# Reciprocal standard deviations in a perceiver kernel: a power on GpSimd in place of ScalarE's root and VectorE's reciprocal

## The chip, the cores and the metric

The kernel runs on one core of a Trainium2 chip, as one program. The metric is the device time of one execution in microseconds (us); lower is better. Five engines work side by side, each with its own queue of instructions in a fixed order: TensorE (PE, with PEld for its weight loads), VectorE (DVE), ScalarE (ACT), GpSimd (POOL) and SyncE (SP, which issues most DMAs). An instruction that depends on another engine waits on a semaphore, and everything behind it in its queue waits too.

## The reference

The input x is 2 x 256 rows of 256 values; a context has 2 x 4096 rows. Twelve sublayers follow one another, each a residual step on the normalised x:

```python
def _layernorm(x, axis=-1, eps=1e-05):
    m = jnp.mean(x, axis=axis, keepdims=True)
    v = jnp.var(x, axis=axis, keepdims=True)
    return (x - m) / jnp.sqrt(v + eps)
...
    x = x + _L0_xattn_ref(_layernorm(x, axis=-1), ctx_1024, ...)
    x = x + _L0_attn_ref(_layernorm(x, axis=-1), ...)
    x = x + _L0_ffn_ref(_layernorm(x, axis=-1), ...)
...
    x = x + _L3_ffn_ref(_layernorm(x, axis=-1), ...)
```

The sublayers are cross attention over the context, self attention, gated and expert feed-forward layers, a state-space layer (l1_attn), an int8 linear layer and a long convolution by Fourier transforms (l2_xattn). Some have norms of their own: the convolution normalises its context projection (twice, once per batch), its query and its gated result (twice); l2_ffn has two RMS norms, `x * rsqrt(mean(x * x) + eps) * w`; l3_attn a layer norm. Each of them needs 1 / sqrt(v + eps) for every row.

## The kernel before

The 512 rows of x lie on the chip as four tiles of 128 rows (partitions) by 256 values. A norm works on a whole tile set: VectorE's `bn_stats` and `bn_aggr` give mean and variance of each row, so the variances of four tiles are a small array of 128 partitions by 4 columns. `rstd` turns it into reciprocal standard deviations `r`: VectorE adds epsilon (L367), ScalarE takes the root in place (L368), VectorE takes the reciprocal (L370). Then VectorE scales the rows with `r`, one column per tile (L384 in `layernorm`), and TensorE transposes the result (L435) for the matmuls. The convolution calls `rstd` on 8 columns (`normalise`) and on 2 columns (`gate`). `norm_of_norm` and `enter` call it twice in a row, because a layer norm is followed directly by another norm: the second variance is worked out from the first one.

That makes twenty calls. By the start of L367 in the profiled execution they stand at 6.6 us (l0_xattn), 140.0 (l0_attn), 229.7 (l0_ffn), 266.3 (l1_xattn), 1248.1 (l1_attn), 1428.0 (the int8 layer), 1455.6 (`normalise(0)`), 1474.7 and 1475.7 (`enter`), 1480.0 (`normalise(1)`), 1517.3 (`gate(0)`), 1535.7 (`gate(1)`), 1547.8 (l2_attn), 1618.0 and 1621.6 (first norm of l2_ffn, a norm of a norm), 1704.4 (its second, `rmsnorm`), 1839.5 (l3_xattn), 2274.5 and 2275.6 (l3_attn), and 2390.3 (l3_ffn).

ScalarE evaluates functions from tables. When the next function is of another set than the one loaded, the compiler puts an ACT_TABLE_LOAD ahead of it in ScalarE's queue. Exp, Silu and the root are each of a set of their own here; copies and Identity need no load.

The order of each engine's instructions is made by a planner when the kernel is built: it simulates the program and, where several instructions are ready on an engine, prefers the one that comes first in the program. Where the author wants another order, `with self.in_order(...)` chains the instructions of the named engines in the order in which they are written. The first cross attentions, the state-space layer and the int8-and-convolution stage name Pool (GpSimd) too; in the other stages GpSimd's order is the planner's.

Between the sublayers TensorE is given other work where there is some: keys and values that later layers need are computed early (`fill`, `early`, `ahead`). ScalarE or VectorE moves their results out of the accumulators (L931, L959, L963), and a DMA stores them (L932, L967).

Names that the prediction's steps touch:
- Convolution stage: L1688 (a maximum over the normalised x of the int8 layer), L1702 (GpSimd, x plus bias), L1776 (filter taps), L1808 (`less`, minus mean times `r`), L1824 (spectrum times filter), L1722 (gain and shift), L1729 (Silu of its feed-forward), L1872, L1884 and L1885 (GpSimd, residual sums).
- Exp and Silu elsewhere: L549 (Exp in l0_xattn), L770 (a dummy Exp that loads the table early, in three self attentions), L1546 (Exp in l1_attn), L1993 (Exp in the router of l2_ffn), L2632 (Exp in l3_attn).
- GpSimd: L457 (x plus a row), L1320 and L2479 (running sums of attention weights), L1455 (a polynomial's first step), L1596 (a product in the state-space layer, read by L1609 on VectorE), L2236 (a sum whose input is VectorE's L2235), L1981 (an iota for the router), L2160 (indirect DMA that sends rows to experts), L2397 (clears a padded tile in l3_xattn).
- L439: gain on a transposed norm.

## Time and profile before

| | |
|---|---|
| time, median of 3 runs (lowest to highest) | 2505.35 us (2504.6 to 2508.54) |
| profiled execution: time, span of its instructions | 2506.37 us, 2504.6 us |
| TensorE busy, granted clock over the span | 2408.0 us (96%), 0.983 |
| VectorE, ScalarE, GpSimd busy | 1691.9 us, 1347.6 us, 912.1 us |
| L367, median of one | 171 ns (16 of the 20) |
| L368, the root, median of one | 206 ns, 20 times |
| L368, table loads | 14 of 1283 ns |
| L370, the reciprocal, median of one | 178 ns, 20 times |
| table loads in all | 32 |

Busy shares are averages over stages with different limits; whether a norm costs time is seen only where it stands. The views used are the page (busy times, the chain of work that ended last, the costliest groups), the view of one source line (durations, what it waits for and who waits for it), the chain in order of time, and the timeline of an engine. In the chain, "issue" is time in which the engine waited for nothing that the profile shows. Times in these views are microseconds from the start of the span.

### The profile page before, as it was taken

The page shows a single profiled execution, that of the slowest core. Times are in us where ns is not written, and L with a number is a line of the kernel's source. Part 1 is how long each engine was busy: PE and PEld are TensorE (multiplying, and loading weights), DVE is VectorE, ACT ScalarE, POOL GpSimd, SP SyncE. Part 2 cuts the span into 40 slices and gives each one's busy share as a digit, 9 for nine tenths or more (in the row PEclk, how much of TensorE's full clock was granted, in tenths as well). Part 3 has the DMA queues.
Part 4 walks back from the last instruction along what each step waited for, and adds up shares of the span by engine and source line. Part 5 has one row for each costly group of instructions (what it writes and reads, how often), then busy time and mean ns, then how long its engine had stood idle before and what let it go on. Part 6 is the DMA issues. An engine that isn't in the chain of part 4 may idle for free.

```text
span 2504.6 us, 51328 instructions
## 1 busy us (share of the span) xinstructions
PE 2408.0 (96%) x20501; PEld 1609.6 (64%) x20501; DVE 1691.9 (68%) x3077; ACT 1347.6 (54%) x2556; POOL 912.1 (36%) x856
## 2 busy tenths in 40 slices
PE   8999999999999999999899998999979999999989
PEld 6865477777766666666633465556945666665678
DVE  5555588888877777777669755554268888854642
ACT  3334576666666666666467422432215777785612
POOL 0520066666666666665539512001011222210010
PEclk9999999999999999999999999999988999999989
DMA  7221433333342222222310102126830000003656
GB/s 301 97 98 67 140 100 96 98 98 94 100 130 69 70 70 71 70 69 69 126 60 1 68 17 97 60 77 216 312 128 1 2 2 2 2 2 136 220 237 218
DMA packets 92638, 243.60 MB, mean 97 GB/s; under 512 B 8072, under 2 KB 23248, under 8 KB 81904
## 3 DMA queue, kind: packets, MB, share of 16 engines
q1 hardware_dynamic: 81088, 219.08, 26.4%
q10 hardware_dynamic: 8784, 13.24, 1.4%
q0 software_dynamic: 2528, 8.00, 0.9%
q8 instruction: 162, 2.65, 0.5%
q14 instruction: 76, 0.62, 0.1%
HBM read 206.87 MB, written 33.42 MB: 96 GB/s over the span
## 4 chain that ended last, share of the span: by engine, by line
PE 89%; DVE 5%; ACT 2%; DMA 2%; issue 1%; POOL 0%; another core or an unknown queue 0%; ACTq 0%; SPq 0%; DVEq 0%; POOLq 0%
PE ps_tr L1238 15%; PE ps_mm L359 13%; PE ps_mm L1285 10%; PE acc L1332 9%; PE ps_tr L2470 5%; PE ps_mm L2430 5%; PE ps_tr L2454 5%; PE acc L359 4%; PE ps_tr L359 2%; PE acc L563 2%; PE acc L1618 2%; PE ps_mm L823 2%; PE ps_mm L1238 2%; DVE mx L2415 1%; PE ps_mm L1577 1%
## 5 line engine op out<-in xcount | busy, mean ns | idle before, releaser
L1320 POOL TENSOR_TENSOR total<-total,S 128x512 f32<-128x512 f32 x434 | 543.1, 1284 | 227.5 <-ACT S L1309 227.0
L1309 ACT ACTIVATE S<-S 128x512 f32<-128x512 f32 x512 | 304.1, 626 | 209.2 <-DVE S L1306 209.0
L1295 DVE TENSOR_TENSOR most<-ps_mm,most 128x512 f32<-128x512 f32 x448 | 278.1, 683 | 101.1 <-ACT S L1292 101.1
L1306 DVE TENSOR_TENSOR S<-S,ps_dec 128x512 f32<-128x512 f32 x512 | 317.3, 678 | 1.7 <-PE ps_dec L1367 1.7
L2434 DVE TENSOR_REDUCE mx<-ps_mm 128x1 f32<-128x512 f32 x448 | 278.1, 683 | 52.1 <-PE ps_tr L2454 48.2
L1292 ACT COPY S<-ps_mm 128x512 f32<-128x512 f32 x512 | 262.4, 598 | 73.2 <-PE ps_mm L1285 73.1
L2458 ACT ACTIVATE PT<-ps_tr 128x512 f32<-128x512 f32 x476 | 246.9, 601 | 82.1 <-PE ps_tr L2454 78.9
L1238 PEld LDWEIGHTS ps_tr<-w_l1x_wv,ctxT 128*64 128x64 f32 x4096 | 236.9, 138 | 46.3 <-issue 41.6
L1285 PE MATMUL ps_mm<-qT,kT 64*128 64x256 f32 x2048 | 256.6, 389 | 0.8 <-DVE qT L1244 0.8
L1332 PE MATMUL acc<-S,v 128*64 128x256 f32 x2048 | 252.2, 385 | 1.7 <-ACT S L1309 1.0
L1238 PE MATMUL ps_tr<-w_l1x_wv,ctxT 128*64 128x128 f32 x4096 | 249.6, 273 | 0.0
L2454 PE MATMUL ps_tr<-qm,kT 32*128 32x256 f32 x1904 | 240.2, 391 | 0.0
L2430 PE MATMUL ps_mm<-kT,qT 32*128 32x512 f32 x896 | 228.9, 627 | 2.9 <-DVE mx L2415 2.7
L1285 PEld LDWEIGHTS ps_mm<-qT,kT 64*128 64x128 f32 x2048 | 188.5, 186 | 44.6 <-issue 12.2
L1332 PEld LDWEIGHTS acc<-S,v 128*64 128x64 f32 x2048 | 139.5, 136 | 96.3 <-ACT S L1292 33.8
L1238 PE MATMUL ps_tr<-ctxT,w_l1x_wk 128*64 128x512 f32 x800 | 189.6, 593 | 0.0
L2454 PEld LDWEIGHTS ps_tr<-qm,kT 32*128 32x128 f32 x1904 | 172.7, 185 | 16.4 <-issue 6.2
L2479 POOL TENSOR_TENSOR sums<-sums,part 128x256 f32<-128x256 f32 x102 | 73.9, 724 | 250.5 <-ACT part L2478 250.5
L2470 PE MATMUL ps_tr<-PT,v 128*32 128x256 f32 x2048 | 139.4, 385 | 0.0
L336 DVE COPY v<-ps_tr 128x512 f32<-128x512 f32 x120 | 82.4, 687 | 44.1 <-PE ps_tr L1238 44.1
L2430 PEld LDWEIGHTS ps_mm<-kT,qT 32*128 32x128 f32 x896 | 80.6, 187 | 48.0 <-issue 41.1
L1238 PEld LDWEIGHTS ps_tr<-ctxT,w_l1x_wk 128*64 128x64 f32 x800 | 59.7, 137 | 70.5 <-issue 58.9
(578 smaller groups left out, 3832.8 us busy)
## 6 DMA issues: line engine op xcount, KB each, us to landing
ctxT<-in_ctxT SPq DMA_DIRECT2D x144, 512.0 KB, 3.6
w_l2f_gu<-in_l2f_gu SPq DMA_DIRECT2D x16, 1024.0 KB, 7.1
bd_dram<-bd SPq DMA_DIRECT2D x8, 1536.0 KB, 6.0
w_l3f_w<-in_l3f_w SPq DMA_DIRECT2D x11, 1028.0 KB, 10.6
w_l3f_w<-in_l3f_w SPq DMA_DIRECT2D x11, 1024.0 KB, 6.8
ctxT<-in_ctxT SPq DMA_DIRECT2D x8, 1024.0 KB, 6.2
ctx<-in_ctx SPq DMA_DIRECT2D x8, 1024.0 KB, 4.8
ahead_ctx<-in_ctxT SPq DMA_DIRECT2D x8, 1024.0 KB, 5.7
```

Source lines behind the costliest of these rows:

```text
L359: self.nc.tensor.matmul(out, lhsT, rhs, start=i == 0, stop=i == len(pairs) - 1)
L1238: nc.tensor.matmul(ps[part], a[:, part], b, start=k == 0, stop=k == len(pairs) - 1)
L1285: nc.tensor.matmul(banks[hh, i][:, j, :], k[part, ts(2 * i + j, P)], q[u][part, :], start=True, stop=True)
L1295: nc.vector.tensor_tensor(m, ps, m, ALU.max)
L1306: nc.vector.tensor_tensor(t, t, spread[u][:, hh, :].unsqueeze(1).to_broadcast([P, 2, L]), ALU.add)
L1309: nc.scalar.activation(t, t, AF.Exp)
L1320: nc.gpsimd.tensor_add(tot, tot, t)
L1332: nc.tensor.matmul(av[u][part], vs[:, 2 * i + j, part], got[hh, i][:, j, :], start=g % 8 == 0 and i + j == 0, stop=g % 8 == 7 and i + j == 2,)
L2430: nc.tensor.matmul(ps, qT[rows, 2 * half + c, ts(t, P)], kT[rows, ts(j, 512)], start=True, stop=True,)
L2434: nc.vector.tensor_reduce(mx[:, c, r, j : j + 1], ps, AX.X, ALU.max)
L2454: nc.tensor.matmul(ps[:, i, :], kT[rows, ts(2 * u + i, P)], q[rows], start=True, stop=True)
L2470: nc.tensor.matmul(ps[ts(r, 32), :], v[:, 2 * u + i, :], pt[:, i, :], start=i == 0, stop=i == 1)
```

## The change

A constant tile of minus one half is written once by VectorE at the start. In `rstd` the sum of variance and epsilon is still made on VectorE, and then GpSimd raises it to the power minus one half in one two-input instruction. ScalarE's root and VectorE's reciprocal are gone, and with them the root's table set. All twenty calls change.

```diff
@@ in Perceiver.__init__
         nc.vector.memset(self.ones, 1.0)
+        self.minus_half = self.const.tile([P, 8], F32, name="minus_half")
+        nc.vector.memset(self.minus_half, -0.5)
         self.ternary = {}
@@ rstd
         nc, n = self.nc, var.shape[1]
-        s = self.sm.tile([P, n], F32, name="std", tag=f"std{n}")
-        nc.vector.tensor_scalar_add(s, var, eps)
-        nc.scalar.sqrt(s, s)
         r = self.sm.tile([P, n], F32, name="rstd", tag=f"rstd{n}")
-        nc.vector.reciprocal(r, s)
+        v = self.sm.tile([P, n], F32, name="std", tag=f"std{n}")
+        nc.vector.tensor_scalar_add(v, var, eps)
+        nc.gpsimd.tensor_tensor(r, v, self.minus_half[:, 0:n], ALU.pow)
         return r
```

## The prediction

> **What bounds the kernel now.** I read the page first: the busy times and the chain that ended last.

> ```profile
> PE 2408.0 (96%) x20501; PEld 1609.6 (64%) x20501; DVE 1691.9 (68%) x3077; ACT 1347.6 (54%) x2556; POOL 912.1 (36%) x856
> ...
> PE 89%; DVE 5%; ACT 2%; DMA 2%; issue 1%; POOL 0%; another core or an unknown queue 0%; ACTq 0%; SPq 0%; DVEq 0%; POOLq 0%
> ```

> TensorE carries 89% of the chain. The change touches no matmul, so it can act only in the few places where TensorE stands still for a norm. ScalarE is no bound (54% busy), so time taken off it is not time gained. Next, the root's own line, L368:

> ```profile
> L368 ACT ACTIVATE std<-std x20: 203/206/208, 6.8 to 2390.5; 128x4 f32<-128x4 f32 x16, 128x8 f32<-128x8 f32 x2, 128x2 f32<-128x2 f32 x2
> L368 ACT ACT_TABLE_LOAD  x14: 1283/1283/1283, 3.4 to 2385.3; - x14
> ```

> Twenty norms on 2, 4 or 8 columns, and 14 table loads. Then the chain in order of time, around each of the twenty. Columns are start, length, who:

> ```profile
> 1474.70 0.18 DVE std L367
> 1474.88 0.02 issue
> 1474.90 0.21 ACT std L368
> 1475.12 0.02 issue
> 1475.14 0.19 DVE rstd L370
> 1475.33 0.02 issue
> 1475.35 0.17 DVE both L1865
> ```

> This is the common form: from the end of the addition of epsilon (L367) to the end of the reciprocal (L370) 0.45 us, with no table load, because the load was already done while ScalarE idled. Only in a few places is the load itself in the chain, as here before l1_attn:

> ```profile
> 1247.64 1.28 ACT L368
> 1248.92 0.01 issue
> 1248.93 0.21 ACT std L368
> 1249.15 0.02 issue
> 1249.17 0.19 DVE rstd L370
> ```

> Here L367 had ended at 1248.22, and the reciprocal ends at 1249.35, 1.13 us later. Last, GpSimd: its rows by form, and its timeline at 1480 us.

> ```profile
> L1320 POOL TENSOR_TENSOR total<-total,S 128x512 f32<-128x512 f32 x434 | 543.1, 1284 | 227.5 <-ACT S L1309 227.0
> L2479 POOL TENSOR_TENSOR sums<-sums,part 128x256 f32<-128x256 f32 x102 | 73.9, 724 | 250.5 <-ACT part L2478 250.5
> L2160 POOL DMA_INDIRECT xs<-xn,slot x12 | 12.1, 1005 | 32.7 <-DVE own L2193 16.1 <-DVE near L2253 13.5 <-issue 3.0
> L1455 POOL TENSOR_SCALAR delta<-low 128x512 f32<-128x512 f32 x2 | 3.0, 1510 | 0.0
> ```

> ```profile
> 1478.43 2.92 POOL L1872 TENSOR_TENSOR add<-add,row_l2x 128x256 f32<-128x256 f32 x4 [18.00 <-issue]
> ```

> **The price of one power.** No row of before shows a power. From below: two-input GpSimd instructions take 724 ns for 256 columns and 1284 ns for 512, so 2.19 ns a column and 0.16 us fixed; four columns of the cheapest operation would be 0.17 us. From above I take the longest GpSimd instruction of the page, 1.51 us. [...] I take 1.0 us for four columns. Scaling what lies over the fixed part, that is 0.6 us for two columns and 1.85 us for eight.

> Handing over: L2236 on GpSimd starts 0.08 us after its VectorE input L2235 ends; L1609 on VectorE starts 0.03 us after L1596 on GpSimd ends. So L367's end to r ready costs 0.11 us plus the power: 1.11 us where 0.45 us was.

> **Removed: table loads.** The 14 loads of the root go. So do 9 more, because without the root the function before was already of the wanted set: L549 (1), L770 (2 of 3), L1546 (1), L1729 (3), L1993 (1), L2632 (1). That leaves 9 of 32. 23 x 1.283 = 29.5 us of ScalarE time, which would be the gain if each were waited for. [...] The trace shows why that is not the gain: most loads begin as soon as ScalarE is idle and end before their input comes. Of the 9 others only one is in the chain, L1729 at 1540.46, and TensorE, still working until 1542.11, resumes at 1542.28: worth 0.17 us.

> **Place by place**, at 1.0 us a power. r means the norm's result.
> - Seven four-column norms on the chain in the common form (6.6, 140.0, 1428.0, 1474.7, 1475.7, 1547.8, 2390.3 us): each 1.11 - 0.45 = +0.66, sum +4.6. The one at 1428 isn't named in the chain, but VectorE goes straight on from it through L1688 to L1776, which the chain has.
> - Two of two columns (1517.3, 1535.7): 0.71 - 0.44 = +0.27 each, +0.5.
> - Eight columns at 1455.6: 1.96 - 0.48, +1.5.
> - Eight columns at 1480.0: in this stage GpSimd's order is written by hand, and the power stands behind the four L1872, which end at 1478.43 + 2.92 = 1481.35, while L367 ended at 1480.70. So r at 1481.35 + 1.85 + 0.03 = 1483.23 instead of 1481.18: +2.05. Queued behind it on VectorE are L1808, L1824 and L1722, for which TensorE waits.
> - 1248.1: 1248.22 + 1.11 = 1249.33 against 1249.35, 0. 1839.5, the same picture: 1839.63 + 1.11 = 1840.74 against 1840.70, 0. The load saved pays for the power.
> - 1704.4 (RMS norm): ScalarE's copy L963, which releases TensorE, no longer stands behind load and root. It can start with its input at 1704.92 instead of 1705.50: -0.6.
> - 1618.0 and 1621.6 (norm of a norm): the first root waits for load and copies, 2.70 us instead of 0.45. But GpSimd clears tiles from 1617.51 to 1620.46. If the first power starts midway at 1619.5, r is there at 1620.5; then 0.60 us as before to the second L367's end and 1.11: 1622.2, as before: 0. Ends -1.6 (no wait, cheap power; TensorE is busy until 1621.4) and +1.0.
> - Off the chain at no cost: 229.7 and 266.3 (TensorE computes early keys; r has about 0.7 and 3.6 us of room), 2274.5 and 2275.6 (TensorE projects positions until 2280.9, about 2.3 us of room). If a power took over 2 us, that cover is gone and they count too.
> - GpSimd already busy with clearing or counting when the power comes, at 140, 1547 and 2390: up to 0.5 us each for the instruction in flight; half of that, +0.75 in all.
> - The constant's memset, 0.1 us at the start on an idle VectorE: 0. L1702, L1884 and L1885, which the power now precedes on GpSimd, have many microseconds before their readers: 0.

> Sum: 4.6 + 0.5 + 1.5 + 2.05 + 0 - 0.6 + 0 - 0.17 + 0.75 = +8.6 us. The profiled execution took 2506.37 us (span 2504.6 and 1.8 around it), 1.0 over the median of 2505.35; so 2515.0 against it, 2514 against the median. At 0.17 us a power the same list gives -1.2 - 0.3 - 0.2 + 0.4 - 0.85 - 0.8 - 0.6 - 1.6 - 0.2 = -5.3; at 1.51 us (two columns 0.84, eight 2.85) 8.1 + 1.0 + 2.5 + 3.1 + 0.5 + 0.5 + 0 + 1.0 - 0.2 + 1.5 = +18. So 17 us for each microsecond of power: zero at about 0.5 us, +5 at 0.8.

> The first GpSimd two-input instruction (L457 at 11.1 us) takes 0.73 us like the later ones, so I charge nothing for a first use. [...]

> About 0.2% (5 us) is what a measurement of this kernel can tell from no change.

> **Rivals.**
> - The power is cheap, near the addition's 0.17 us: up to 5.3 us faster, 2500. For it: the same kind of instruction on GpSimd. [...] It decides below 0.2 us; from there to 0.8 us nothing is measurable.
> - The power runs value by value. As a stand-in a column costs the longest instruction, 1.5 us: 6, 3 and 12 us. The list gives about +40 (seven), +5, +12, +12, +5, +5, +3, +9, and about +16 from the places that lose their cover: +107, 2612. No row excludes it.
> - The power is queued behind a GpSimd instruction that waits. L1981 waits until 1709.87 and L2397 until 1844.5; if the planner puts the powers of 1704.4 and 1839.5 behind them, r comes some 5 us late at each. At the first, L439 waits for a DMA until 1709.6 anyway, so about +3; at the second +5: 2522. Against: both norms precede them in the program.

> **How the numbers follow.** Forecast (0.8 to 2.5 us a power, slower) 0.50; cheap 0.30, of which faster 0.09 and same 0.21; queued 0.07; value by value 0.13. Slower 0.70, same 0.21, faster 0.09. The range runs from 2500 to 2560, that is +55 or near 4 us a power; what is beyond is most of the last case and a little below. The forecast's own range is 2510 to 2545.

> **What would show it.** Right: 9 table loads instead of 32; a GpSimd row of 20 powers near 1 us; VectorE waiting some 1.1 us between L367's successor and xn; TensorE's gaps at 140, 1456, 1517 and 2390 longer by 0.3 to 1.5 us, those at 1248 and 1840 unchanged. Wrong: powers under 0.5 or over 2.5 us, or a power that starts long after its input.

## The result, and the profile after

The changed kernel takes 2529.14 us (median of four runs, 2526.81 to 2531.78). The kernel before took 2504.97 us beside it (four runs, 2502.39 to 2508.54). The ratio is 1.0096, with a 95% interval of 1.0084 to 1.0108: slower by 24 us, inside the range on record and with its sign, but nearly three times the +8.6 us of the sum. The profiled execution has a span of 2528.7 us where 2504.6 was, 24.1 more, and TensorE's granted clock over it is 0.976 where 0.983 was.

First the page of after, busy times and the chain that ended last.

```profile
PE 2420.3 (96%) x20499; PEld 1614.6 (64%) x20501; DVE 1691.6 (67%) x3058; ACT 1314.0 (52%) x2513; POOL 931.9 (37%) x876
...
PE 35%; DVE 3%; DMA 1%; issue 1%; POOL 1%; ACT 1%; DVEq 0%; ACTq 0%; POOLq 0%; SPq 0%
```

ScalarE lost 33.6 us of work (1347.6 to 1314.0), which is the 23 table loads at 1.283 us and the 20 roots at 0.2, and GpSimd gained 19.8. TensorE does the same matmuls and is busy 12.3 us longer: a first sign that they ran more slowly. The chain's shares add up to 42% because it is followed back only to 1488 us, where it reaches GpSimd additions for whose start the profile shows no releaser. Next, the line of the power, and GpSimd's and VectorE's way to it:

```profile
L371 POOL TENSOR_TENSOR rstd<-std,minus_half x20: 706/1026/1648, 6.9 to 2412.6; 128x4 f32<-128x4 f32 x16, 128x8 f32<-128x8 f32 x2, 128x2 f32<-128x2 f32 x2
```

Smallest, median, largest: 0.71 us for two columns, 1.03 for four, 1.65 for eight. The timeline of VectorE shows who waits for it (in brackets the idle time before the instruction, and what ended it):

```profile
1253.68 0.41 DVE L385 TENSOR_SCALAR xn<-xres,bmv,rstd 128x256 f32<-128x256 f32 x1 [1.21 <-POOL rstd L371]
...
1484.27 0.16 DVE L1866 TENSOR_TENSOR both<-bmv,rstd 128x4 f32<-128x4 f32 x1 [1.13 <-POOL rstd L371]
...
1492.55 0.17 DVE L1809 SCALAR_TENSOR_TENSOR less<-bmv,rstd 128x8 f32<-128x8 f32 x1 [2.29 <-POOL rstd L371]
```

The first answers the place at 1248 us of before, the second `enter`, the third `normalise(1)`. The chain in order of time shows the power queued, at that last place and at the last norm:

```profile
1487.99 2.33 POOL add L1873 x4
1490.32 0.56 issue
1490.88 1.65 POOL rstd L371
...
2412.39 0.25 POOL tiles_at L2113
2412.64 1.02 POOL rstd L371
```

At the last norm the power starts 1.04 us after the addition of epsilon, twice the most that the list allowed for GpSimd being busy; the rest is much as forecast. What was not in the sum is in TensorE's rows. The granted clock has only two values, 1.0 and 0.5. In every profiled execution the stretches at 0.5 begin on a grid of 3.41 us and last a multiple of that; where the grid lies against the program differs from execution to execution. In the profiled execution of before they add up to 84.9 us, in that of after to 121.4 (2 us of each lie behind the last instruction). The convolution stage shows why. TensorE's timeline of before, at its three longest pauses there:

```profile
1456.87 1.01 PE L359 MATMUL ps_tr<-w,xqT 128*128 128x256 bf16 x4 [3.21 <-DVE y L1710]
...
1484.55 7.13 PE L359 MATMUL ps_mm<-yT,w_l2x_w1a 128*128 128x512 f32 x16 [2.16 <-DVE yT L1722]
...
1518.53 0.33 PE L1721 MATMUL ps_tr<-ident,xn 128*128 128x128 f32 x1 [2.74 <-DVE xn L1851]
```

And of after:

```profile
1465.29 1.01 PE L361 MATMUL ps_tr<-w,xqT 128*128 128x256 bf16 x4 [4.46 <-DVE y L1711]
...
1495.88 4.64 PE L361 MATMUL ps_mm<-yT,w_l2x_w1a 128*128 128x512 f32 x5 [4.09 <-DVE yT L1723]
...
1533.25 0.47 PE L1722 MATMUL ps_tr<-ident,xn 128*128 128x128 f32 x1 [3.37 <-DVE xn L1852]
```

In before half clock sets in at the first of the three only (from 1455.8, for 6.8 us). In after it sets in at all three. Windows of after, with TensorE's busy time and matmuls, then the clock (PEclk), DMA share and GB/s:

```profile
1434.00:1578.00 144.00, 124.52 (x434) 0.91 0.20 74
...
1463.90:1470.70 6.80, 4.83 (x15) 0.50 0.00 1
1494.60:1501.40 6.80, 5.52 (x7) 0.50 0.00 0
1532.20:1539.00 6.80, 5.42 (x9) 0.50 0.00 0
```

The same stage of before:

```profile
1430.00:1560.00 130.00, 116.89 (x432) 0.96 0.21 77
```

Half clock does not go with the length of a pause alone, but with how little TensorE does within one stretch of the grid. Here are the stretches of 3.41 us on the grid at these pauses, the first three rows of before and the others of after:

```profile
1452.38:1455.79 3.41, 1.28 (x7) 1.00 0.00 0
1483.10:1486.51 3.41, 1.97 (x5) 1.00 0.00 0
1517.23:1520.64 3.41, 1.71 (x7) 1.00 0.00 0
```

```profile
1460.49:1463.90 3.41, 0.34 (x3) 1.00 0.00 0
1491.21:1494.62 3.41, 0.58 (x2) 1.00 0.00 0
1528.76:1532.17 3.41, 1.12 (x3) 1.00 0.00 0
```

TensorE was busy for 1.28 us of the first, and half clock follows; for 1.97 and 1.71 us of the next two, and it does not; for 0.34 to 1.12 us in after, and it does. Counted over the fourteen profiled executions, from 20 us on:

| TensorE busy in a grid stretch at full clock | stretches | half clock in the next |
|---|---|---|
| under 40% | 101 | 101 |
| 40 to 60% | 185 | 91 |
| over 60% | 9553 | 18 |

(The first 20 us are left out: the clock's record begins 12.0 us into before and 13.2 us into after.) So a longer pause makes half clock more likely, and the place of the grid has a part in it.

To see where the 24 us arise, I matched every matmul of after with the same one of before and took how much later it starts. By stretch (times of before):

| stretch | places | on record | measured | half clock, before to after |
|---|---|---|---|---|
| start to 220 | 6.6, 140 | +1.6 | +4.2 | 0 to 3.4 us |
| 220 to 1420 | 230, 266, 1248 | 0 | +1.0 | 17.1 to 17.0 |
| 1420 to 1450 | 1428 | +0.7 | +2.0 | 0 to 3.4 |
| 1450 to 1560 | 1456 to 1547 | +6.1 | +11.6 | 10.2 to 23.9 |
| 1560 to 1760 | 1618, 1621, 1704 | -0.6 | +3.7 | 6.8 to 17.0 |
| 1760 to 2380 | 1839, 2274, 2275 | 0 | -1.4 | 30.7 to 27.3 |
| 2380 to end | 2390 | +0.9 | +3.1 | 20.0 to 29.2 |

Where half-clock time was added, the stretch costs 1.3 to 5.5 us more than the list says; where none was added, it differs by 1.0 and 1.4. That is a correlation in two executions, and the experiments test it.

One more thing shows in the first stretch. The four VectorE instructions that write the normalised x took 2.31 us in before, 3.23 in after, and only 1.38 where nothing runs beside them (at 7.28 us in before). In before, GpSimd's clears of the attention's tiles had run for 1.5 of their 3.5 us when these four began; now the power stands ahead of the small ones (0.1 to 0.6 us each), and all of them fall on xn.

### The profile page after: what moved, and what is told of

Its sections match the earlier page's. It is cut to its first block, busy times and chain, and to the rows that moved or that the text cites. A ratio compares the mean times of both kernels' runs of the same rounds, so it can differ in the third digit from the quotient of the medians.

```text
span 2528.7 us, 51273 instructions
## 1 busy us (share of the span) xinstructions
PE 2420.3 (96%) x20499; PEld 1614.6 (64%) x20501; DVE 1691.6 (67%) x3058; ACT 1314.0 (52%) x2513; POOL 931.9 (37%) x876
## 3 DMA queue, kind: packets, MB, share of 16 engines
q0 software_dynamic: 2528, 8.00, 0.9%
## 5 line engine op out<-in xcount | busy, mean ns | idle before, releaser
L2455 PEld LDWEIGHTS ps_tr<-qm,kT 32*128 32x128 f32 x1904 | 171.8, 185 | 16.1 <-issue 6.2
```

What stands on the lines that cost most here:

```text
L2455: nc.tensor.matmul(ps[:, i, :], kT[rows, ts(2 * u + i, P)], q[rows], start=True, stop=True)
```

## The experiments

Theory A: the longer wait for each norm costs its own length, as listed, and besides it lengthens TensorE's pauses, so that the clock is halved more often. Theory B, in several forms: GpSimd's occupation itself, or the waits alone, cost the rest, and the clock only goes along. Ratios are to the kernel before, run beside it.

**1. A cheap instruction in the power's place.**

```diff
-        nc.vector.memset(self.minus_half, -0.5)
+        nc.vector.memset(self.minus_half, 0.5)
...
-        nc.vector.tensor_scalar_add(v, var, eps)
-        nc.gpsimd.tensor_tensor(r, v, self.minus_half[:, 0:n], ALU.pow)
+        nc.vector.tensor_scalar(v, var, 1e-6, eps, ALU.mult, ALU.add)
+        nc.gpsimd.tensor_tensor(r, v, self.minus_half[:, 0:n], ALU.add)
```

> The changed kernel with the power replaced by an addition in the same GpSimd instruction (the norms' values are left out: every reciprocal deviation comes out near one half). Same queues, same hand-overs, same 23 table loads gone; only the instruction's own time shrinks, from 1.03 us to about 0.2 us for four columns. Theory A (the loss is the length of the wait: directly about +9, and the rest because TensorE's longer pauses let its granted clock fall to one half): the whole loss goes, 2497 to 2503 us, 2 to 8 us under the kernel before, with no more half-clock time than before (about 85 us). Theory B (the 15 us above the direct sum come from using GpSimd at all: its queue, the hand-over, sharing with VectorE): some 15 us of loss stay, 2517 to 2523 us.

Measured: 2510.64 us (10 runs), ratio 1.0014 [1.0004, 1.0023]. The instruction took 0.20 us, and some 20 of the 24 us went. Neither expectation fits: the power's length is most of the cost, yet the kernel did not become faster than before. Two causes of what remained can be read from the trace. The small clears now fall on xn altogether, and GpSimd's additions of L458, queued behind them, on its last two instructions (timeline of VectorE of this kernel):

```profile
140.76 4.08 DVE L385 TENSOR_SCALAR xn<-xres,bmv,rstd 128x256 f32<-128x256 f32 x4 [0.32 <-POOL rstd L371]
```

4.08 us instead of 2.31. And a half-clock stretch follows at 145 us that before has not. So a cheap power on GpSimd, put in the same places, would gain nothing either.

**2. The wait without GpSimd.** The kernel before, with three multiplications by one on VectorE ahead of ScalarE's root.

```diff
         nc.vector.tensor_scalar_add(s, var, eps)
+        for _ in range(3):
+            nc.vector.tensor_scalar_mul(s, s, 1.0)
         nc.scalar.sqrt(s, s)
```

> The kernel before (root on ScalarE, reciprocal on VectorE, 32 table loads) with three multiplications by one on VectorE between the addition of epsilon and the root: some 0.6 us more wait in each norm, hidden at the four places where the root waits for ScalarE anyway. No GpSimd. Direct sum: 12 norms on the path x 0.6 = +7 us. Theory A: the pauses pass about 3 us in the same places as in the changed kernel (near 1455, 1482 and 1515 us), the clock falls there too, and the loss is +12 to +24 us, 2517 to 2529. Theory B: +7 or less, 2508 to 2512, half-clock time as before.

Measured: 2529.98 us, ratio 1.0090 [1.0071, 1.0109], 1 us over the upper edge of A and far from B. But the added wait was not the 0.6 us that was meant. A multiplication took 0.17 us at quiet places and up to 0.65 us at others. At the eleven norms that the list has in full on the path (seven common, two of two columns, two of eight) the wait grew by 11.4 us in all, where the power's grew by 9.3. So about as much added wait costs about as much without a power on GpSimd; which share of it is the clock, the total does not tell. It isn't the same loss place by place either: 6.4 of the 20.5 us in its trace lie between 220 and 1180 us and between 1612 and 1650, where the power itself cost 1 us or less, since there ScalarE's root and its table load are still in the way.

The convolution stage tells more. Its seven norms waited 6.3 us longer than in before (in after 5.7), but half clock there stayed at 10.2 us, and the stage gave only +5.7 us, about the wait itself; in after half clock rose to 23.9 and the stage gave +11.6. One of its pauses, 3.40 us from 1492.18 us, has no half clock behind it. It fell into two stretches of the grid:

```profile
1490.72:1494.13 3.41, 1.46 (x4) 1.00 0.00 0
1494.13:1497.54 3.41, 1.96 (x5) 1.00 0.00 0
```

**3. The power twice** (a second one, by one).

```diff
-        nc.gpsimd.tensor_tensor(r, v, self.minus_half[:, 0:n], ALU.pow)
+        nc.gpsimd.tensor_tensor(v, v, self.minus_half[:, 0:n], ALU.pow)
+        nc.gpsimd.tensor_tensor(r, v, self.ones[:, 0:n], ALU.pow)
```

> The changed kernel with a second power (by one) behind the first on GpSimd: another 1.0 us or so in each norm (0.7 with two columns, 1.6 with eight). Direct sum on about 16 norms: +17 us over the changed kernel. Theory A: +17 and more half-clock time again, +20 to +35 over the changed kernel, 2549 to 2564. Theory B: no extra use of another kind, so +17, 2546. If hidden norms keep their cover, a little less in both.

Measured: 2552.61 us, ratio 1.0177 [1.0160, 1.0194]. By the ratios that is 20 us more than after, for 1.0 us more of power and 0.1 of hand-over; the prediction's slope of 17 us per us makes 19 of it. The time falls among A's numbers, but half-clock time did not rise further (118.8 us in its profile), so this run does not show the clock at work. Between 220 and 1180 us it is 4.7 us later, where after was level: the cover at 230 and 266 us is used up (some 1.8 us), and two stretches of half clock that after has not, at 280 and 321 us, cost the other 2.9.

**4. Keeping TensorE busy in the pauses: four kernels that were wrongly fitted.** If half clock follows from pauses, matmuls whose result nobody reads should prevent it.

```diff
+    def warm(self, rhs, n):
+        ps = self.bank([P, 512], "tr")
+        for _ in range(n):
+            self.nc.tensor.matmul(ps[:, 0 : rhs.shape[1]], self.ident, rhs, start=True, stop=True)
```

> The changed kernel with idle matmuls (their result is read by nobody) in three pauses of the convolution stage: 14 of 512 columns behind normalise(0), 15 before the spectrum's second half after normalise(1), 20 of 256 columns in gate(0), 4 in gate(1); at full clock 0.22 and 0.11 us each. The norms' waits stay as they are. Theory A: the half-clock spans near 1464, 1495 and 1532 us of the changed kernel (three of 6.83 us) vanish and with them 5 to 10 us: 2519 to 2524. Theory B: nothing gained, 2529, or a little more where the idle matmuls outlast the pause.

Measured: 2563.76 us, ratio 1.0216 [1.0198, 1.0234]. It tests nothing: one such matmul of 512 columns in f32 takes 0.88 us (two rows of 0.44), four times the 0.22 on record (in l0_ffn of before, matmuls of 512 columns in bf16 start 0.216 us apart), and some read tiles that the norm itself makes, so that they could not lie in the pause: TensorE stood still for up to 8.4 us. The second kernel, for which I still counted half of the 0.88, read constants, 9, 8 and 6 matmuls, ahead of `normalise(0)` and of the first steps of `enter` and `gate(0)`:

> The changed kernel with idle matmuls on a constant (result read by nobody, 0.43 us each at full clock) queued on TensorE in the three pauses of the convolution stage: 9 ahead of normalise(0), 8 after normalise(1), 6 in gate(0), each set a little shorter than the pause that the changed kernel has there (4.46, 4.09 and 3.37 us). All waits for the power stay. Theory A (clock): the three half-clock spans at about 1464, 1495 and 1532 us go, 20 us less half-clock time, and 7 to 10 us of time with it: 2519 to 2523. If the clock were only a companion of the loss (theory B): 2529 as the changed kernel, or up to 2 us more.

Measured: 2529.96 us, ratio 1.0090 [1.0075, 1.0105], no gain. But the three half-clock stretches of the stage were gone in its trace, and the matmuls behind the second and third of these places made up 2.9 and 3.1 us against after. It was given back: the idle work lasted 7.9, 7.0 and 5.3 us, longer than the pauses. The same on the kernel before, with 6, 4 and 5:

> The kernel before with idle matmuls in the same three pauses, 6, 4 and 5 of them (its pauses there are 3.21, 2.16 and 2.74 us). Theory A: the one half-clock span it has there (1456 us, 6.8 us long) goes, and 2 to 3 us with it: 2503 to 2505. Theory B: 2507 or a little more.

Measured: 2514.47 us, ratio 1.0023 [1.0014, 1.0032]. And with three more groups in l3_ffn:

> As the kernel before with idle matmuls in the convolution stage, and further ones at the start of l3_ffn, where the kernel before has half clock from 2394 to 2411 us: 8 of 256 columns that read the last residual tile, 5 behind the router's logits, 12 behind the counting of rows. Theory A: half-clock time falls by up to 10 us more, 2498 to 2503. If the planner puts them where they stand in the way of real matmuls, slower by up to 3 us instead.

Measured: 2515.98 us, ratio 1.0028 [1.0018, 1.0038], though the clock was higher (0.986 where before had 0.983, medians). A higher clock that is bought with over-long idle work costs more than it gives.

**5. The power only where table load or root stood in the way**: the first norm of l2_ffn's pair and its RMS norm; elsewhere root and reciprocal.

```diff
+        if power:
+            nc.gpsimd.tensor_tensor(r, s, self.minus_half[:, 0:n], ALU.pow)
+            return r
         nc.scalar.sqrt(s, s)
```

> The kernel before with the power on GpSimd at two norms only: the first of l2_ffn's norm of a norm (1618 us) and the RMS norm (1704 us), where the root waits for ScalarE's copies and its own table load. Direct: -1.6 at the first at best (there the second root still needs its table, now loaded while GpSimd works), -0.6 at the second: 2504 to 2507 us, with no change of the half-clock time beyond its scatter. Theory B (any power on GpSimd costs elsewhere) would have it above 2508.

Measured: 2508.72 us, ratio 0.9999 [0.9990, 1.0008]. No gain was seen, and the interval leaves room for 0.1% at most. In the trace the matmuls gain 0.1 us at the first place, where TensorE is busy meanwhile, and 0.5 at the second; a half-clock stretch at 1623 us, which before has not, takes 1.6.

**6. Idle matmuls that fit.** Pieces of 256 columns (0.44 us each) into the pauses themselves: behind the int8 layer's first pair of matmuls, ahead of w1a, and ahead of `gate(0)`'s transposes; the total of each group stays below the pause.

```diff
             self.mm(ps[:, t % 2, :], [(xT[:, k, ts(t, P)], w[:, k, :]) for k in range(KC)])
+            if t == 0:
+                self.idle(9, "acc")
...
                 transform(0, 1, 1)
+                self.idle(8, "acc")
...
                 transform(1, 1, 0)
+                self.idle(6, "tr")
```

> The kernel after, with matmuls whose result nobody reads, of 256 columns (about 0.44 us each), put into three of TensorE's pauses and sized to end before them: 9 in the pause of 4.46 us behind the first pair of the int8 layer's matmuls (4.0 us of work), 8 in the one of 4.09 us ahead of the w1a matmuls (3.5 us), 6 in the one of 3.37 us ahead of gate(0)'s transposes (2.6 us). A: the pauses lower TensorE's clock, and the lowered clock is about half of the missing time: the half-clock spans of 6.8 us behind these three pauses vanish, each is worth some 3 us, and the time is 2518 to 2524 us. B: the clock only goes along with the waits, the waits themselves cost the time: 2527 to 2532 us as without them.

TensorE's timeline of this kernel at the three places:

```profile
1463.61 4.05 PE L361 MATMUL acc<-fz,ident 128*128 128x256 f32 x18
...
1492.45 3.62 PE L361 MATMUL acc<-fz,ident 128*128 128x256 f32 x16
1496.71 3.70 PE L366 MATMUL ps_mm<-yT,w_l2x_w1a 128*128 128x512 f32 x8 [0.64 <-DVE yT L1730]
...
1527.79 2.75 PE L361 MATMUL ps_tr<-fz,ident 128*128 128x256 f32 x12
```

The idle work ends before the norm's result comes (0.64 us of pause are left at w1a). The clock of the stage, window as for after:

```profile
1434.00:1578.00 144.00, 133.21 (x494) 0.95 0.21 77
```

Measured: 2523.58 us (six runs, 2515.53 to 2530.53), ratio 1.0051 [1.0035, 1.0066] where after had 1.0096 [1.0084, 1.0108]. A holds for the stage. The norms are those of after, TensorE does more work, and yet the kernel is faster. The three stretches are gone, and half-clock time in the stage (the table's row from 1450 us) is 10.2 us, as in before. The stage then costs +7.3 us against before instead of +11.6; the list has +6.1. So 13.7 us of half clock were worth 4.3 us here, 0.3 us each. The profiled execution is the slowest of the six, and as a whole it is no faster than that of after (2530.53 and 2530.52 us): what the stage gains is lost to other stretches of half clock, at 1239, 1256, 1283 and 1641 us. The ratio's gain, some 11 us, is more than this stage's, and where the rest comes from is open; three of the six runs lie in the range of B. So the firm part of this test is the stage in the trace.

The kernel before with 6, 4 and 5 pieces:

> The kernel before with the same idle matmuls, cut to its shorter pauses: 6 in 3.21 us, 4 in 2.16 us, 5 in 2.74 us. A: of the three only the first has a half-clock span of 6.8 us behind it, worth some 3 us: ratio to the kernel before 0.998 to 1.0. B: no gain, ratio 1.0.

Measured: 2504.85 us (11 runs), ratio 0.9987 [0.9978, 0.9996]. A again: in its trace the stage has no half clock left, and the matmuls behind it start 3.7 us earlier than in before.

**7. The clears behind xn.** In the first self-attention, a small copy that reads the last of xn is put ahead of GpSimd's clears.

```diff
+        clears = ExitStack()
+        if not interleaved:
+            clears.enter_context(self.in_order(mybir.EngineType.Pool))
+            nc.gpsimd.tensor_copy(v[:, 0, 0, 16:17], xn[:, NT - 1, 0:1])
         nc.gpsimd.memset(v[:, :, :, 16:32], 0.0)
```

> The kernel after, with GpSimd's clears of the first self-attention's pads and values held back until the normalised x is written (one small GpSimd copy reads it ahead of them). If these clears are what slows the four VectorE instructions that write xn at 142 us, the four take 1.4 us instead of 3.2 us and the matmuls behind come 1.5 to 2 us earlier; the time is 2526 to 2528 us. If not, they still take 3.2 us and the time stays at 2529 us.

VectorE's timeline, first of after, then of this kernel:

```profile
142.40 3.23 DVE L385 TENSOR_SCALAR xn<-xres,bmv,rstd 128x256 f32<-128x256 f32 x4 [1.14 <-POOL rstd L371]
```

```profile
143.09 1.38 DVE L385 TENSOR_SCALAR xn<-xres,bmv,rstd 128x256 f32<-128x256 f32 x4 [1.14 <-POOL rstd L371]
```

The clears, with the additions queued behind them, were the cause: 1.38 us. Against after, the matmuls behind gain 3.7 us between 140 and 150 us, of which 1.85 is xn; the half-clock stretch at 146 us is gone too, and another one at 312 us takes 1.6 us back. In time: 2528.35 us, ratio 1.0071 [1.0056, 1.0086]. The interval touches that of after, so the size is known from the trace only.

**8. The two together, on the kernel before.**

> The kernel before with the fitted idle matmuls of the run before and the clears held back behind xn in the first self-attention: root and reciprocal stay on ScalarE and VectorE. The four xn instructions take 1.4 us where they took 2.31, so 0.9 us more than the idle matmuls alone: ratio to the kernel before 0.9978 to 0.999. If the clears cost nothing on the path, 0.9987 as with the idle matmuls alone. The two differ by less than the interval is wide, so the trace's matmul starts around 145 us have to tell them apart.

Measured: 2500.92 us (11 runs), ratio 0.9984 [0.9975, 0.9993]. xn takes 1.38 us, and the matmuls at 144 us start 0.9 us earlier than with the idle matmuls alone. That is the fastest version here, 4 us below before; whether it beats the idle matmuls alone the intervals don't tell.

## Why the prediction was right in sign and wrong in size

**The price of the power was right.** 1.03, 0.71 and 1.65 us were measured where 1.0, 0.6 and 1.85 were taken. That is 0.155 us for a further column, where the prediction's two-input rows have 2.19 ns. The 1.0 us was an estimate between the 0.17 and the 1.51 us on record: no run of before shows it for a power, and 1.03 us, measured in after, stands in its place. From the end of the addition of epsilon to r ready it is 1.10 to 1.13 us at the common places, 1.11 on record. The rivals of a cheap power and of one that costs 1.5 us a column fall with the row of L371. No power was queued behind a waiting GpSimd instruction at 1704 and 1839, so the third rival did not occur either.

**The list of places was nearly right.** Nine table loads are left, as counted. At 1248 the wait is 1.17 us from epsilon to r where 1.12 was, at 1839 it is 1.13 where 1.07 was: no gain, no loss. `normalise(1)` waits 2.26 us with the four additions ahead of it (the list has 2.53). At 1618 the clears did not hold up the power, which starts 0.09 us behind epsilon, but TensorE was busy until then as forecast, and nothing was gained. Two terms were too small: at 2390 the power stands behind the last of eight clears and counts, so TensorE's pause grows by 1.55 us (3.99 where 2.44 was) instead of 0.9; and in the first self-attention xn is stretched by 0.9 us, for which the list had nothing. The step that failed there is "GpSimd already busy ... half of that": I asked what delays the power, not what the power delays on GpSimd and where that then falls.

With the rows of after in place of those taken, the same list gives about +10.1 us (five common places 3.4, xn 0.9, the two `normalise` 1.25 and 1.78, the gates 0.7, l2_attn 1.2, l3_ffn 1.55, less 0.7 for the load and the RMS norm).

**The step that failed is that the sum had no term for the clock.** "What bounds the kernel now" says that the change can act only where TensorE stands still, and then charges each pause its own added length. Some 14 of the 24.2 us are not length of pauses. They stand against 36.5 us more of half clock, 0.39 us for each. Other readings give about the same: 0.32 and 0.36 in the convolution stage when the stretches were taken out of after and of before (experiment 6), 0.41 between 1650 and 1690 us (10.2 us of half clock, 4.2 us later), and 0.31 from run to run over the repeated runs of all these kernels (within each kernel, 163 runs). At 0.31 to 0.41 the 36.5 us are worth 11 to 15 us: the clock can carry the 14, but up to 3 us of them may be something else. That the pauses bring half clock, and that it costs its share, is shown in the convolution stage: by experiment 6, and from the other side by experiment 2, where much the same waits without more half clock cost about their own length. For the rest of the kernel it is inferred from the same pattern. The data was on the page: before's clock was 0.983, one pause of its convolution stage brought half clock, and the two others left their stretches of the grid only 50 and 58% busy.

That the time fell into the forecast's range of 2510 to 2545 is luck in part. The range was made for powers of 0.8 to 2.5 us; by the list a loss of 24 us would have needed one of 1.9 us, and it took 1.03.

A stretch of the grid need not be idle throughout to bring half clock: from 20 us on, all 101 stretches under 40% busy were followed by it (one in before, at 1452 us, was busy for 1.28 of 3.41 us). Nor does the length of a pause decide alone: pauses of 3.21 us in before and 3.37 in after brought 6.8 us at half clock, and one of 3.40 in experiment 2, cut in two by the grid, brought none.

**What stays open.** Not every stretch follows a pause. The one of 10.2 us at 1679 us comes after pieces of 32 rows with pauses below 0.7 us, in a stretch of the grid that was about 80% busy (eight of the table's 18 are this place); it is absent from the profile of before, of experiments 2, 3, 5 and 8 and of the second kernel of 6, but present in the two variants of before with over-long idle work, which have no power. What decides it was not shown; I guess that it is the grid's phase, and then part of the 24.2 us of the two profiled executions may be that of the pair compared; over the repeated runs, half clock worked out from each run's clock, 2 x (1 - clock) x span, has a median of 114 us for after and 85 for before, an increase of 29 rather than 36.5. What decides between 40 and 60% was not found. Why experiment 1 lost another 2.7 us in the convolution stage than the list allows at 0.2 us a power was not followed up.

## What to carry to other kernels

Before lengthening a wait of the engine that carries the chain, look at its clock and at how busy it stays in each stretch of the clock's grid around the wait: here waits longer by 10 us in all cost 24. An engine that idles is no free place for a short instruction on the path, if the instruction takes longer there or a queue stands in front of it (here 1.11 us to the result where 0.45 was, and 1.04 us of queue at the last norm); removing 33.6 us of ScalarE work gained almost nothing (0.7 us by the list), because ScalarE was waited for at few places. Idle matmuls in a pause paid where they ended before the pause did (1.0051 where after had 1.0096, and 0.9987 on the kernel before), and gave nothing or cost time where they didn't (1.0090, and 1.0023 and 1.0028).
